# Layer 1's self-attention in a new order: queries half a head earlier, the last value matmul behind the next scores

## The chip, the cores and the metric

The kernel runs on one core of one Trainium2 chip. A core has five engines that each work through a queue of their own in order: TensorE (PE, with the weight load PEld), VectorE (DVE), ScalarE (ACT), GpSimd (POOL) and SyncE (SP, which here only starts transfers). They wait for each other through semaphores. The metric is the device time of one execution in microseconds (us); of several runs the median is given.

## The reference

The program is a decoder of two layers with layer normalisation after each residual addition. The residual x is 4 batches x 512 positions x 512 features in float32. Layer 0 has self-attention with 8-wide heads, a cross-attention and a mixture of eight experts; layer 1 has self-attention, cross-attention with 32 heads, and a quantised gated FFN. The change touches layer 1's self-attention alone:

```python
xqkv = x @ Wqkv                                  # 512 -> 16 query heads, 4 key heads, 4 value heads of 128
xq, xk = apply_rotary_emb(xq), apply_rotary_emb(xk)
xk, xv = repeat(xk, 4), repeat(xv, 4)            # four query heads share one key and value head
scores = einsum('bqhd,bkhd->bhqk', xq, xk) * 128 ** -0.5 + causal_mask
attn = einsum('bhqk,bkhd->bqhd', softmax(scores), xv)
x = layernorm(x + attn.reshape(B, S, 2048) @ Wo)
```

## The kernel before

The residual lies in SBUF for the whole run, as 16 tiles X[t] of 128 positions x 512 features. `l1_attn` (from line 887) takes 64 heads in order, 16 for each of the four batches, and works with the residual of a batch turned round: `st["xt"]`, features by positions, made by `transposed` (L258, 16 transposes of 128x128, copied by ACT and DVE in turn, L262 and L260).

For one head n these are the steps:

- `queries(n, i)` (L933): four matmuls, i = 0 to 3, each adding 128 features, into one PSUM bank of `ps_m`; after the last one `rope` rotates: three DVE operations (L903 to L905) and one POOL addition (L906). `keys(n)` does the same for every fourth head, all in one (L160 and `rope`).
- `scores(n, qi)` (L946): a matmul for the 128 queries qi against the (qi + 1) * 128 keys that the causal mask leaves, so 512, 384, 256 or 128 columns; then mask (L947) and negated maximum (L948) on DVE, and the exponential with its sum on ACT (L950).
- `normalise(n, qi)` (L956, L957): reciprocal and multiplication on DVE, SBUF to SBUF.
- `turn(n, c)` (L963): transposes of the probabilities' block column c into a bank of `ps_t`, copied to the tile PT by ACT for even c (L968), by DVE for odd c (L966).
- `values(n, pts)` (L978): four matmuls over PT into a bank of `ps_m`, copied by ACT (L980) to one quarter of the tile attnT; after every fourth head `add_projection` multiplies by Wo (16 matmuls, L160) and DVE adds to X (L313).

A float32 matmul shows in the trace as two, so a "pair" in this document is one matmul of the program. PSUM has three banks for scores (`ps_s`), two for transposes (`ps_t`), three for all else (`ps_m`).

The main loop has three heads in flight: in head n it transposes the probabilities of n and multiplies them by the values, computes the scores of n + 1, and the queries of n + 2. Its four inner steps are scores, one query matmul, one turn; `values` follows whole. At the end of a head come, where they are due: the next batch's transposes (`h == 13`), `at_start` (for n = 0, 1, 2: `finish(n + 1)`, the last part of layer 0's FFN for batch n + 1: scaling on ACT and DVE, L867 and L868, transposes L872, `add_projection` with 8 matmuls, layer normalisation), `at_end` (the first steps of the cross-attention, in the last five heads), and after the 16th head `layernorm` and `prep_values`.

The order in which an engine sees the instructions is fixed when the program is built. In this stage a scheduler sets it: an instruction may overtake others on its engine when they are not ready by the scheduler's own reckoning, with the order of the program as the priority. So in the kernel before, the first query matmul or key matmul of the next head often stands ahead of a head's last value matmul. The cross-attention behind the stage, in turn, is written out in a fixed order by a table of steps (`plan`, `todo`), which the change leaves alone.

Of the kernel before, what the change touches and what calls it, by code (L numbers as in the profile page):

```python
# [17 lines left out]
P = 128  # L18
B, S, F = 4, 512, 512
# [67 lines left out]
def decoder_kernel(ctx: ExitStack, tc: tile.TileContext, a: dict, out: bass.AP):  # L87
# [21 lines left out]
    V, A, G, PE = nc.vector, nc.scalar, nc.gpsimd, nc.tensor  # L109


    def act(tag, free, bufs=1, dtype=F32):
        return ap.tile([P, *free], dtype, tag=tag, name=tag, bufs=bufs)
# [13 lines left out]
    def pst(dtype=F32):  # L127
        if "ps_t" not in pools:
            return psm(dtype)
        return pools["ps_t"].tile([P, 512], dtype, tag="t", name="ps_t")  # L130

    def psm(dtype=F32):
        return pools["ps_m"].tile([P, 512], dtype, tag="m", name="ps_m")
# [16 lines left out]
    def tk(t):  # L150
        return slice(t * P, (t + 1) * P)
# [15 lines left out]
    ident = kc[:, C_ID:C_ID + P]  # L167
# [22 lines left out]
    X = []  # L190
# [55 lines left out]
    def layernorm(b):  # L246
        for i in range(4):
            tile_moments(b, i)
        table_roots(b)
        for i in range(4):  # L250
            normalise_tile(b, i)

    def transposed(b):
        xt = act("xT", [4, S])
        for k in range(4):
            pt = pst()
            for t in range(4):
                PE.transpose(pt[:, tk(t)], X[4 * b + t][:, tk(k)], ident)  # L258
            if k % 2:
                V.tensor_copy(xt[:, k, :], pt)  # L260
            else:
                A.copy(xt[:, k, :], pt)  # L262
        return xt
# [44 lines left out]
    def add_projection(b, lhs, rhs):  # L308

        for t in range(4):  # L310
            ps = psm()
            mm(ps, [x[:, tk(t)] for x in lhs], rhs)
            V.tensor_tensor(X[4 * b + t], X[4 * b + t], ps, ALU.add)  # L313

    def chunks(w):
        return [w[:, k, :] for k in range(w.shape[1])]
# [5 lines left out]
    def l0_attn(xt0):  # L322
# [82 lines left out]

        N = len(pairs)
        for n in range(2):
# [8 lines left out]
        for n, (b, m) in enumerate(pairs):  # L416
            for step in range(4):
                turn(n, step, 0)
                if n + 1 < N:
                    scores(n + 1, step)  # L420
                turn(n, step, 1)
                if n + 2 < N:
                    project(n + 2, step)
                if n + 1 < N and step:
                    normalise(n + 1, step - 1)
# [3 lines left out]
            values(n)  # L429
            if n + 1 < N:  # L430
                normalise(n + 1, 3)
# [455 lines left out]
    def l1_attn(at_start, at_end):  # L887
        cos, sin = prob("cos", [S], 1), prob("sin", [S], 1)
        causal_mask = prob("mask", [P], 1)
        nc.sync.dma_start(causal_mask, a["k_cols"][:, C_MASK:C_MASK + P])  # L890
        nc.sync.dma_start(cos, a["k_rope"][0])
        nc.sync.dma_start(sin, a["k_rope"][1])
        wqkv = rows(a["L1_attn_Wqkv"])
        wk = load(wqkv[:, :, 4 * F:5 * F], (4, F))
        wv = load(wqkv[:, :, 5 * F:6 * F], (4, F))
        wq, wo = [None] * 4, [None] * 4
        for of, g in ((wq, 0), (wq, 1), (wo, 0), (wq, 2), (wo, 1), (wq, 3), (wo, 2), (wo, 3)):
            src = wqkv[:, :, g * F:(g + 1) * F] if of is wq else rows(a["L1_attn_Wo"])[:, 4 * g:4 * g + 4, :]
            of[g] = load(src, (4, F))

        def rope(dst, ps, scale):
            x, y = tmp(), tmp()
            V.scalar_tensor_tensor(x, ps, scale, cos, ALU.mult, ALU.mult)  # L903
            V.scalar_tensor_tensor(y[0:64], ps[64:128], scale, sin[64:128], ALU.mult, ALU.mult)
            V.scalar_tensor_tensor(y[64:128], ps[0:64], scale, sin[0:64], ALU.mult, ALU.mult)  # L905
            G.tensor_tensor(dst, x, y, ALU.add)  # L906

        heads = [(b, h) for b in range(B) for h in range(H1)]  # L910
        st, qs, ks, ps_q, ps_sm = {}, {}, {}, {}, {}

        def prep_values(b):
            v = prob("v", [4, F], 1)
            for t in range(4):
                ps = psm()
                mm(ps, [st["xt"][:, k, tk(t)] for k in range(4)], chunks(wv))
                A.copy(v[:, t, :], ps)
            st["v"] = v

        def keys(n):
            b, h = heads[n]
            if h % 4 == 0:
                ps = psm()
                mm(ps, [wk[:, k, tk(h // 4)] for k in range(4)], chunks(st["xt"]))
                ks[b, h // 4] = prob("k", [S], 3)
                rope(ks[b, h // 4], ps, 1.0)

        def queries(n, i):
            b, h = heads[n]  # L930
            if i == 0:
                ps_q[n] = psm()
            PE.matmul(ps_q[n], lhsT=wq[h // 4][:, i, tk(h % 4)], rhs=st["xt"][:, i, :],  # L933
                      start=(i == 0), stop=(i == 3))
            if i == 3:
                qs[n] = prob("q", [S], 3)
                rope(qs[n], ps_q.pop(n), float(D1) ** -0.5)

        def scores(n, qi):
            b, h = heads[n]  # L940
            w, q, k = (qi + 1) * P, qs[n], ks[b, h // 4]
            if qi == 3:
                ps_sm[n] = [None] * 4, small(4, "sums", 3), small(4, "nmax", 3)
            probs, sums, nmax = ps_sm[n]
            s = pss()
            PE.matmul(s[:, :w], lhsT=q[:, tk(qi)], rhs=k[:, :w], start=True, stop=True)  # L946
            V.tensor_tensor(s[:, tk(qi)], s[:, tk(qi)], causal_mask, ALU.add)  # L947
            V.tensor_reduce(nmax[:, qi:qi + 1], s[:, :w], AX.X, ALU.max, negate=True)  # L948
            p = probs[qi] = prob("P", [S], 8)
            A.activation(p[:, :w], s[:, :w], AF.Exp, bias=nmax[:, qi:qi + 1],  # L950
                         accum_out=sums[:, qi:qi + 1])

        def normalise(n, qi):
            probs, sums, _ = ps_sm[n]
            p, w = probs[qi], (qi + 1) * P
            V.reciprocal(sums[:, qi:qi + 1], sums[:, qi:qi + 1])  # L956
            V.tensor_scalar(p[:, :w], p[:, :w], sums[:, qi:qi + 1], None, ALU.mult)  # L957

        def turn(n, c):
            probs = ps_sm[n][0]  # L960
            pt = pst()
            for qi in range(c, 4):
                PE.transpose(pt[:, tk(qi)], probs[qi][:, tk(c)], ident)  # L963
            sb = prob("PT", [S], 6)
            if c % 2:
                V.tensor_copy(sb[:, c * P:], pt[:, c * P:])  # L966
            else:
                A.copy(sb[:, c * P:], pt[:, c * P:])  # L968
            return sb

        def values(n, pts):
            b, h = heads[n]
            g = h // 4
            if h % 4 == 0:
                st["ft"] = act("attnT", [4, S])
            av = psm()
            for c in range(4):
                PE.matmul(av[:, c * P:], lhsT=st["v"][:, c, tk(g)], rhs=pts[c][:, c * P:],  # L978
                          start=(c == 0), stop=(c == 3))
            A.copy(st["ft"][:, h % 4, :], av)  # L980
            if h % 4 == 3:
                add_projection(b, chunks(st["ft"]), chunks(wo[g]))
            del ps_sm[n]

        N = len(heads)
        st["xt"] = transposed(0)
        for n in range(2):
            keys(n)
            for i in range(4):
                queries(n, i)  # L990
        for qi in (3, 2, 1, 0):
            scores(0, qi)
        prep_values(0)
        for qi in (3, 2, 1, 0):
            normalise(0, qi)
        for n, (b, h) in enumerate(heads):
            pts = []
            if n + 2 < N:
                keys(n + 2)
            for i in range(4):  # L1000
                qi = 3 - i
                if n + 1 < N:
                    scores(n + 1, qi)
                if n + 2 < N:
                    queries(n + 2, i)
                pts.append(turn(n, i))
                if n + 1 < N and i:
                    normalise(n + 1, qi + 1)
            values(n, pts)
            if n + 1 < N:  # L1010
                normalise(n + 1, 0)
            if h == 13 and b + 1 < B:
                st["xt"] = transposed(b + 1)
            if n < 3:
                at_start(n)
            if n >= N - 5:
                at_end(n - N + 5)
            if h == 15:
                layernorm(b)
                if b + 1 < B:  # L1020
                    prep_values(b + 1)

# [476 lines left out]
```

## Time and profile before

| | |
|---|---|
| median of 3 runs | 2916.74 us (2912.76 to 2916.99) |
| the profiled execution | 2925.97 us |
| its span, first to last instruction | 2924.2 us |
| mean granted TensorE clock | 0.983 |
| layer 1's self-attention, from its first key matmul to its last projection | about 980 to 1970 us |
| its queries, L933 | 512 matmul records, 261.4 us busy, 594 ns each |
| its scores, L946 | 512 matmul records, 183.3 us busy, 441 ns each |
| its values, L978 | 512 matmul records, 162.8 us busy, 441 ns each |
| DVE multiplication by the reciprocal, L957 | 256, 152.0 us busy, 594 ns each |
| POOL's last step of the rotation, L906 (queries) | 64, 82.0 us busy, 1281 ns each |

A row of a wait names the waiting engine, its tile and line, then the engine, tile and line that ended the wait; its numbers are the total in us, how many times, and the longest. A row of the timeline has start, duration, engine, line, operation, tiles and shape; "x2" merges two records, and brackets hold the idle time before and what ended it. A row of a stretch has the length, then for PE, PEld, DVE, ACT and POOL the busy time and the number of instructions, then PE's granted clock, the DMA engines' share and GB/s. A row of a group has its shape, the count, busy us and mean ns, and the idle time before.

### The profile page before, as it was taken

To read this page: it belongs to the slowest core of one execution; us is meant where nothing else is said; L and a number is where in the kernel's file an instruction comes from. 1 tells how busy PE (TensorE), PEld (TensorE's weight loads), DVE (VectorE), ACT (ScalarE), POOL (GpSimd) and SP (SyncE) were. 2 spreads that over 40 slices of the span, in tenths; PEclk is the share of its full clock that TensorE was granted. 3 is DMA by queue.
4 is the path that set the end of the run, shared out by engine and by line. 5 is a ranking of instruction groups with operands and counts; after the bars stand their busy time and mean duration, and the time that the engine had idled before them with its cause. 6 is when DMAs were issued, how large, how long until landed. Compare 5 with 4: busy or idle time off the path is not lost. (4 is left out here: it accounts for less than half of the span.)

```text
span 2924.2 us, 30438 instructions
## 1 busy us (share of the span) xinstructions
PE 2763.2 (94%) x11434; PEld 1347.8 (46%) x11434; DVE 1757.1 (60%) x3551; ACT 1046.8 (36%) x1929; POOL 425.0 (15%) x436
## 2 busy tenths in 40 slices
PE   8999999998998889999999999999999999998987
PEld 3444444565665345555555555553334334334443
DVE  4565564553111476767667666756656666565998
ACT  2333342333221122232233223234555554554443
POOL 3000000042002100111101101123333232211000
PEclk9999999999999899999999999999999999999999
DMA  9700000004322120000000001111111020010000
GB/s 386 278 15 1 15 4 27 23 29 137 101 85 97 35 87 1 1 0 1 1 1 1 1 0 44 58 47 38 56 55 58 37 86 27 12 51 1 15 15 30
DMA packets 61128, 142.76 MB, mean 49 GB/s; under 512 B 6537, under 2 KB 26010, under 8 KB 54818
## 3 DMA queue, kind: packets, MB, share of 16 engines
q1 hardware_dynamic: 54818, 123.80, 11.8%
q0 software_dynamic: 6144, 16.79, 1.6%
q8 instruction: 99, 1.62, 0.2%
q14 instruction: 67, 0.55, 0.1%
HBM read 84.73 MB, written 47.45 MB: 45 GB/s over the span
## 5 line engine op out<-in xcount | busy, mean ns | idle before, releaser
L1182 DVE TENSOR_REDUCE maxes<-ps_b 128x2 f32<-128x1024 f32 x256 | 312.6, 1223 | 212.0 <-PE ps_b L1194 113.8
L160 PE MATMUL ps_m<-w,attnT 128*128 128x512 f32 (+1 forms) x992 | 391.8, 547 | 9.7 <-DVE x L313 9.7
L1198 ACT ACTIVATE PT<-ps_b 128x1024 f32<-128x1024 f32 x256 | 260.3, 1023 | 237.0 <-PE ps_b L1194 236.9
L1178 PE MATMUL ps_b<-k,q 32*128 32x512 f32 x1024 | 287.0, 642 | 6.8 <-ACT PT L1198 6.8
L1194 PE MATMUL ps_b<-q,k 32*128 32x512 f32 x1024 | 285.5, 642 | 1.4 <-DVE maxes L1182 1.4
L933 PE MATMUL ps_m<-xT,w 128*128 128x512 f32 x512 | 261.4, 594 | 0.0
L313 DVE TENSOR_TENSOR x<-x,ps_m 128x512 f32<-128x512 f32 x128 | 87.8, 687 | 284.5 <-PE ps_m L160 257.1
L160 PEld LDWEIGHTS ps_m<-w,attnT 128*128 128x128 f32 x736 | 141.2, 195 | 177.3 <-issue 162.8
L950 ACT ACTIVATE P<-ps_s,nmax 128x512 f32<-128x512 f32 (+3 forms) x256 | 135.4, 529 | 234.9 <-DVE nmax L948 233.8
L946 PE MATMUL ps_s<-k,q 128*128 128x512 f32 (+3 forms) x512 | 183.3, 441 | 19.1 <-POOL q L906 17.4
L906 POOL TENSOR_TENSOR q<-tmp 128x512 f32<-128x512 f32 x64 | 82.0, 1281 | 765.8 <-DVE tmp L905 731.2
L978 PE MATMUL ps_m<-PT,v 128*128 128x512 f32 (+3 forms) x512 | 162.8, 441 | 4.0 <-DVE PT L966 4.0
L370 ACT ACTIVATE P<-ps_s,nmax 128x512 f32<-128x512 f32 x128 | 88.5, 693 | 203.5 <-DVE nmax L368 203.5
L957 DVE TENSOR_SCALAR P<-P,sums 128x512 f32<-128x512 f32 (+3 forms) x256 | 152.0, 594 | 5.3
L1178 PEld LDWEIGHTS ps_b<-k,q 32*128 32x128 f32 x1024 | 76.5, 183 | 155.2 <-issue 141.1
L160 PE MATMUL ps_m<-w,xT 128*128 128x512 f32 (+1 forms) x384 | 143.8, 530 | 3.4 <-DVE v L338 3.4
L1205 PE MATMUL ps_m<-PT,vv 128*32 128x512 f32 x1024 | 137.5, 609 | 7.5 <-ACT PT L1198 7.5
L963 PEld LDWEIGHTS ps_t<-kc,P 128*128 128x128 f32 x640 | 84.0, 141 | 121.3 <-issue 82.0
L978 PEld LDWEIGHTS ps_m<-PT,v 128*128 128x128 f32 x512 | 89.0, 190 | 106.1 <-issue 48.8
L348 PE MATMUL ps_m<-xT,w 128*128 128x512 f32 x256 | 122.3, 605 | 10.4 <-DMA w<-in_L_attn_Wq 10.4
L948 DVE TENSOR_REDUCE nmax<-ps_s 128x1 f32<-128x512 f32 (+3 forms) x256 | 125.5, 490 | 5.6
L947 DVE TENSOR_TENSOR ps_s<-ps_s,mask 128x128 f32<-128x128 f32 x256 | 75.1, 294 | 81.1 <-PE ps_s L946 78.9
(281 smaller groups left out, 4403.7 us busy)
## 6 DMA issues: line engine op xcount, KB each, us to landing
hidden<-w SPq DMA_DIRECT2D x16, 1024.0 KB, 16.7
result<-w SPq DMA_DIRECT2D x16, 1024.0 KB, 16.3
w<-in_L_ffn_gateT SPq DMA_DIRECT2D x8, 1024.0 KB, 4.8
tmp<-tmp POOLq DMA_DIRECT2D x64, 128.0 KB
w<-in_L_ffn_upT SPq DMA_DIRECT2D x8, 1024.0 KB, 4.8
w<-in_L_ffn_downT SPq DMA_DIRECT2D x8, 1024.0 KB, 5.5
w<-in_L_attn_Wqkv SPq DMA_DIRECT2D x6, 1024.0 KB, 8.9
w<-in_L_attn_Wo SPq DMA_DIRECT2D x5, 1024.0 KB, 13.6
```

The costliest lines, as they stand in the source:

```text
L160: PE.matmul(ps, lhsT=x, rhs=y, start=(i == 0), stop=(i == n - 1))
L933: PE.matmul(ps_q[n], lhsT=wq[h // 4][:, i, tk(h % 4)], rhs=st["xt"][:, i, :], start=(i == 0), stop=(i == 3))
L946: PE.matmul(s[:, :w], lhsT=q[:, tk(qi)], rhs=k[:, :w], start=True, stop=True)
L948: V.tensor_reduce(nmax[:, qi:qi + 1], s[:, :w], AX.X, ALU.max, negate=True)
L950: A.activation(p[:, :w], s[:, :w], AF.Exp, bias=nmax[:, qi:qi + 1], accum_out=sums[:, qi:qi + 1])
L957: V.tensor_scalar(p[:, :w], p[:, :w], sums[:, qi:qi + 1], None, ALU.mult)
L978: PE.matmul(av[:, c * P:], lhsT=st["v"][:, c, tk(g)], rhs=pts[c][:, c * P:], start=(c == 0), stop=(c == 3))
L1178: PE.matmul(s[:, j, :], lhsT=q[strip(i), tk(qi)], rhs=k[strip(i), :], start=True, stop=True)
L1182: V.tensor_reduce(at[:, 2 * half:2 * half + 2, 16 * (1 - g % 2)], s, AX.X, ALU.max, negate=True)
L1194: PE.matmul(s[:, j, :], lhsT=k[strip(i), tk(c)], rhs=q[strip(i), :], start=True, stop=True)
L1198: A.activation(p, s, AF.Exp)
L1205: PE.matmul(avs[g][strip(i), :], lhsT=vv[c][:, 4 * m + i, 16 * par:16 * par + 32], rhs=pts[g, c, i // 2][:, i % 2, :], start=(c == 0), sto ...
```

## The change

Four things are moved; what is computed stays the same.

- The queries run half a head further ahead. Before the loop two query matmuls of the third head are issued, and inner step i issues query matmul (i + 2) % 4 of head n + 2 + i // 2: in head n the last two of head n + 2, then the first two of head n + 3.
- `values` becomes a generator: it issues the first three value matmuls and stops; the rest (last value matmul, copy, projection, and after the 16th head layer normalisation and the next batch's values) runs in the next head, behind its first scores.
- The next batch's transposes move from the end of the 14th head into its last two inner steps, two groups of four in each, through a new function `turn_residual`.
- `layernorm` and `prep_values` move from the loop into `values`.

The diff (a hunk that adds one empty line is left out):

```diff
@@ -971,28 +972,51 @@
         def values(n, pts):
             b, h = heads[n]
             g = h // 4
+            av = psm()
+            for c in range(4):
+                if c == 3:
+                    yield
+                PE.matmul(av[:, c * P:], lhsT=st["v"][:, c, tk(g)], rhs=pts[c][:, c * P:],
+                          start=(c == 0), stop=(c == 3))
             if h % 4 == 0:
                 st["ft"] = act("attnT", [4, S])
-            av = psm()
-            for c in range(4):
-                PE.matmul(av[:, c * P:], lhsT=st["v"][:, c, tk(g)], rhs=pts[c][:, c * P:],
-                          start=(c == 0), stop=(c == 3))
             A.copy(st["ft"][:, h % 4, :], av)
             if h % 4 == 3:
                 add_projection(b, chunks(st["ft"]), chunks(wo[g]))
+            if h == 15:
+                layernorm(b)
+                if b + 1 < B:
+                    prep_values(b + 1)
             del ps_sm[n]
 
+        def turn_residual(b, k):
+            if k == 0:
+                st["xt"] = act("xT", [4, S])
+            pt = pst()
+            for t in range(4):
+                PE.transpose(pt[:, tk(t)], X[4 * b + t][:, tk(k)], ident)
+            if k % 2:
+                V.tensor_copy(st["xt"][:, k, :], pt)
+            else:
+                A.copy(st["xt"][:, k, :], pt)
+
         N = len(heads)
-        st["xt"] = transposed(0)
+        for k in range(4):
+            turn_residual(0, k)
         for n in range(2):
             keys(n)
             for i in range(4):
                 queries(n, i)
+        for i in range(2):
+            queries(2, i)
         for qi in (3, 2, 1, 0):
             scores(0, qi)
         prep_values(0)
         for qi in (3, 2, 1, 0):
             normalise(0, qi)
+
+
+        rest = iter(())
         for n, (b, h) in enumerate(heads):
             pts = []
             if n + 2 < N:
@@ -1001,24 +1025,26 @@
                 qi = 3 - i
                 if n + 1 < N:
                     scores(n + 1, qi)
-                if n + 2 < N:
-                    queries(n + 2, i)
+                if i == 0:
+                    next(rest, None)
+                if h == 13 and b + 1 < B and i >= 2:
+                    turn_residual(b + 1, 2 * i - 4)
+                    turn_residual(b + 1, 2 * i - 3)
+                if n + 2 + i // 2 < N:
+                    queries(n + 2 + i // 2, (i + 2) % 4)
                 pts.append(turn(n, i))
                 if n + 1 < N and i:
                     normalise(n + 1, qi + 1)
-            values(n, pts)
+            rest = values(n, pts)
+            next(rest)
             if n + 1 < N:
                 normalise(n + 1, 0)
-            if h == 13 and b + 1 < B:
-                st["xt"] = transposed(b + 1)
+            else:
+                next(rest, None)
             if n < 3:
                 at_start(n)
             if n >= N - 5:
                 at_end(n - N + 5)
-            if h == 15:
-                layernorm(b)
-                if b + 1 < B:
-                    prep_values(b + 1)
```

## Prediction

> **What bounds the kernel now.** I read the page's first part, then stretches of the span, then TensorE's waits inside the changed stage, then the timeline of one head. The first line says that TensorE (PE) is busy for nearly the whole span; the stretches show that this holds inside layer 1's self-attention (about 975 to 1970 us) too:
>
> ```profile
> PE 2763.2 (94%) x11434; PEld 1347.8 (46%) x11434; DVE 1757.1 (60%) x3551; ACT 1046.8 (36%) x1929; POOL 425.0 (15%) x436
> ...
> 975.00:1110.00 135.00, 119.72 (x338) 57.68 (x337) 83.51 (x190) 35.55 (x80) 10.39 (x8) 0.95 0.16 55
> 1110.00:1960.00 850.00, 831.78 (x2762) 440.42 (x2761) 576.99 (x1380) 254.16 (x689) 103.14 (x84) 1.00 0.04 12
> ```
>
> From 1110 to 1960 us PE is busy for 831.78 of 850 us at clock 1.00, so a change of order, with the same matmuls, can win little more than the holes. Who ends the holes, in that stretch and then in 975 to 1110 us:
>
> ```profile
> PE ps_s L946 <- POOL q L906: 16.6, 29, 0.6
> PE ps_m L978 <- DVE PT L966: 1.2, 4, 0.3
> ...
> PE ps_t L963 <- ACT PT L968: 5.2, 2, 3.3
> PE ps_t L872 <- DVE w L868: 3.4, 2, 1.7
> PE ps_m L978 <- DVE PT L966: 2.8, 4, 1.0
> ```
>
> The first score matmul of every second head waits for its rotated queries. In one such head, PE first, then VectorE (DVE):
>
> ```profile
> 1316.89 2.10 PE L978 MATMUL ps_m<-PT,v 128*128 128x512 f32 x6
> 1318.83 1.02 PE L933 MATMUL ps_m<-xT,w 128*128 128x512 f32 x2
> 1319.69 0.38 PE L978 MATMUL ps_m<-PT,v 128*128 128x128 f32 x2
> 1320.64 1.13 PE L946 MATMUL ps_s<-k,q 128*128 128x512 f32 x2 [0.57 <-POOL q L906]
> 1321.60 0.60 PE L963 MATMUL ps_t<-kc,P 128*128 128x128 f32 x4
> ...
> 1317.05 0.69 DVE L903 SCALAR_TENSOR_TENSOR tmp<-ps_m,cos 128x512 f32<-128x512 f32 x1
> 1318.46 0.68 DVE L905 SCALAR_TENSOR_TENSOR tmp<-ps_m,sin 64x512 f32<-64x512 f32 x1
> 1319.18 0.29 DVE L966 COPY PT<-ps_t 128x128 f32<-128x128 f32 x1
> 1319.38 1.35 DVE L957 TENSOR_SCALAR P<-P,sums 128x256 f32<-128x256 f32 x1
> 1321.80 0.30 DVE L947 TENSOR_TENSOR ps_s<-ps_s,mask 128x128 f32<-128x128 f32 x1 [0.68 <-PE ps_s L946]
> ```
>
> The last query matmul of the coming head is issued at the head's end; three DVE operations (1317.05 to 1319.14) and POOL's 1.27 us addition follow, and scores cannot start before 1320.64. Starts tell more than the idle column, because matmul ends are modelled: a pair of 128-column matmuls takes 0.22 us from start to start (that at 1303.24 is followed at 1303.46), here 0.95. So 0.73 us is lost, and the score pair itself takes 0.96 instead of 0.86: 0.83 us a time. The rotation stands ahead of the 128-column copy of PT as well, which is why the last value matmul comes late.
>
> **The change, part by part.** In the changed kernel no matmul, vector operation, copy or DMA is added or removed; PE's order differs, and with it that of DVE and ScalarE (ACT).
>
> *Queries half a head ahead: gain 25.7 us.* The last query matmul of a head is now its second of four, about half a head before the scores that need it. The wait of L946 for POOL happens 31 times (29 in the long stretch, 2 before): 31 x 0.83 = 25.7. If only the idle of the row goes, 17.4; that is the lower end.
>
> *Last value matmul behind the next scores: gain 6.5 us.* Its wait for PT is short: at 1306.37 a pair starts, the value pair follows at 1307.30 where 1307.23 was due, and takes 0.32 where 0.22 is due, 0.17 in all. Some 30 heads make 5; the rows of 2.8 and 1.2 us contain a few long ones, so I put 6.5 (ends 4 and 9). What now hides the copy is the 0.86 us score pair. If this cover is gone, the 0.17 us returns, and the waiting matmul holds up the projection of every fourth head, which stands behind it on PE.
>
> *DVE in the heads without key or output projection, two in four: cost 2.4 us.* Here PE needs: 3.44 for four query pairs, 2.16 scores, 2.16 values, 1.1 for ten transposes, 8.86 us. By start-to-start steps DVE needs four masks 1.32, four maxima 1.64, reciprocals 0.76, normalisations 1.21, rotation 2.11, copies 0.67, together 7.71, and it must wait about 0.95 for the first exponential of the head, which stands before the second mask in the new order: 8.66. I followed one such head by hand: the copy of PT ends 0.5 us ahead of the last value matmul, the last normalisation 0.6 ahead of the first transpose. So it just fits. After a key projection DVE starts the next head 1.25 us late and misses the value matmul by about 0.15: 16 groups x 0.15 = 2.4. With full durations instead of steps (8.21 + 0.97 = 9.18 us) each light head loses 0.32 less some slack, 0.5 a group, 8 us: the upper end; the lower is 0.
>
> [...] The row:
>
> ```profile
> L957 DVE TENSOR_SCALAR P<-P,sums 128x128 f32<-128x128 f32 x59 | 50.3, 853 | 2.1
> L957 DVE TENSOR_SCALAR P<-P,sums 128x256 f32<-128x256 f32 x59 | 37.9, 642 | 1.1
> ```
>
> The shortest 128x128 takes 285 ns, an undisturbed 128x256 350: while POOL adds, DVE loses 0.57 + 0.29 = 0.86 us a head. [...] If the row's 0.86 stays and falls on the last normalisation, its 0.6 us of slack is overrun by 0.26, 64 times: 17 us, and the sum below would be 0. [...]
>
> *PSUM banks in the first two heads: cost 6.7 us.* ps_m has three. Across the head's end the half-built queries now hold one and the unfinished values another; finish(1) and finish(2) project between, four tiles through one bank, and each tile waits for DVE's addition to the tile before. One gap: 0.20 from the end of a matmul stream to DVE (1321.60 to 1321.80), 0.69 addition (row L313), 0.22 back to PE (copy end 1319.47 to 1319.69) = 1.11. Three gaps twice: 6.7. Ends 3 (the queue of PE hides part) and 9 (DVE is delayed further). For finish(3) values and scores interleave with its transposes: 2 us, ends -1 and 5.
>
> *The same two heads otherwise: gain 3, cost 1.6.* The rotation no longer stands before DVE's scaling of w (L868), for which PE waits 3.4 us: 3 gained, ends 0 and 6. The PT copy of the second transpose now stands behind the rotation while DVE is catching up after layer normalisation: 0.8 twice lost.
>
> *Batch ends: cost 4.5 us.* The 16 transposes of the next batch's residual move into the 14th head and share two ps_t banks with the probabilities; four of them wait for a copy, and the first query matmul behind them waits for ACT. The nearest row, the old transposes, lost about 0.5 a time; four waits of 0.5, less the old one, make 1.5, three times. Ends 0 and 9. Layer normalisation and the values of the next batch move one score pair later: 0, hidden behind 16 matmul pairs of 0.86 us. The three or four last heads have half a head of queries less to fill them while DVE limits: 1, ends 0 and 1.7.
>
> The DMAs and POOL's operations stay in their order. The sum: -25.7 - 6.5 - 3 + 2.4 + 6.7 + 2 + 1.6 + 4.5 + 1 = -17.0. The cross-attention's order behind is the same and PE leads there too, so the whole stage moves forward. The profiled execution took 2925.97 (span 2924.2), 9.2 above the median of 2916.74; its span should become 2907, the median 2916.7 - 17.0 = 2899.7, in round numbers 2900.
>
> [...] The page's row of clocks has all tenths but one at 9 here, yet the stretch 975 to 1110 has 0.95: 0.05 x 135 = 7 us of clock lost already. [...] I take 0 and keep 7 for the range.
>
> **The rivals.**
> *A wait takes its place (0.15).* The first transposes of a head then wait for the last normalisation as scores did for queries; half of the 25.7 is lost, 2912.6 at most, 2909 if some of the batch-end cost hides. For: 6.9 us of weight loads already wait for L957. Against: 0.6 us of slack by hand.
> *DVE becomes the bound (0.12), slower.* [...] It decides once a light head's DVE chain exceeds 8.86 + 17/32 = 9.4 us. Against: DVE was busy for 577 of 850 us, blocking included.
> *Nothing moves (0.05), 2917.* The time returns at the cross-attention's start, which waits for loads. Against: PE has no DMA wait there, and those loads move at 0.13 to 0.18 of the DMA engines.
> *All new costs hide (0.08).* -25.7 - 6.5 = -32: 2885.
>
> **How the numbers follow.** My sum has 0.60, with its own range 2892 to 2908 (its unknown terms added as independent). A measurement tells 0.2%, 5.8 us, from no change: faster is below 2910.9. Faster: 0.60 + 0.08 + about half of the 0.15 = 0.75; same: the rest of it and 0.05 = 0.13; slower 0.12. The range runs from 2885 to 2914, leaving out the slower rival and small ends.
>
> **What would show it.** The row L946 <- POOL q near 0; L957 128x128 near 300 ns; new rows of L160 (ctx) waiting for DVE x before 1070 us, about 7 us; waits of the batch-end transposes; 1110 to 1960 shorter by some 25 us. Wrong it is if L963 waits for P in most heads, or if L979's wait for PT grows in the light heads.

## The result and the profile after

The changed kernel takes 2880.96 us (median of 4 runs, 2878.24 to 2889.82), the kernel before beside it 2916.23 (4 runs): ratio 0.9887, 95% interval 0.9864 to 0.9909. That is 35.3 us less. The prediction had the sign right and the size wrong: 2900, with a range down to 2885. The profiled execution took 2881.12 us, its span 2879.3.

TensorE's and VectorE's totals, and the same two stretches of the span (columns: stretch, length, then busy time of PE, weight loads, DVE, ACT and POOL with their instructions, PE clock, DMA share, GB/s):

```profile
PE 2747.5 (95%) x11434; PEld 1347.1 (47%) x11434; DVE 1700.2 (59%) x3551; ACT 1048.1 (36%) x1929; POOL 427.3 (15%) x436
...
975.00:1110.00 135.00, 120.51 (x352) 58.31 (x351) 86.38 (x216) 39.88 (x98) 9.95 (x8) 0.94 0.13 47
1110.00:1960.00 850.00, 846.96 (x2863) 449.69 (x2861) 532.27 (x1377) 261.70 (x686) 125.25 (x109) 1.00 0.04 15
```

In the long stretch PE is now busy for 846.96 of 850 us (831.78 before), and the cross-attention behind the stage begins at 1928 us instead of 1975. The stretch thus holds 32 us of cross-attention now; in what is left of it, 1110 to 1928 us, PE is busy for 815.4 of 818. DVE's total fell from 1757.1 to 1700.2 us with the same 3551 instructions.

TensorE's waits in 1110 to 1960 us, and then in 975 to 1110 us:

```profile
PE ps_t L997 <- ACT xT L1001: 1.4, 3, 0.5
PE ps_m L1152 <- DVE x L313: 0.8, 1, 0.8
...
PE ps_m L160 <- DVE x L313: 5.5, 7, 0.8
PE ps_t L964 <- ACT PT L969: 4.7, 2, 3.6
PE ps_m L979 <- ACT PT L969: 1.6, 2, 0.9
PE ps_t L872 <- DVE w L868: 1.2, 2, 1.0
```

(Lines of the stage moved by 1, the part behind it by 26: the scores are now L947, the normalisation L958.) The row of scores waiting for POOL's q, 16.6 us in 29 waits, is gone. New are the predicted waits of L160 for the additions to x in the first heads, 5.5 us in 7, and one wait of 0.5 at each batch end.

One head of the changed kernel, the one behind that which answers to the head shown before (some rows left out), PE first, then DVE:

```profile
1302.01 1.02 PE L934 MATMUL ps_m<-xT,w 128*128 128x512 f32 x2
1302.87 0.27 PE L964 MATMUL ps_t<-kc,P 128*128 128x128 f32 x1
1302.98 2.10 PE L979 MATMUL ps_m<-PT,v 128*128 128x512 f32 x6
1304.92 1.02 PE L947 MATMUL ps_s<-k,q 128*128 128x512 f32 x2
1305.77 0.38 PE L979 MATMUL ps_m<-PT,v 128*128 128x128 f32 x2
...
1300.56 0.68 DVE L903 SCALAR_TENSOR_TENSOR tmp<-ps_m,cos 128x512 f32<-128x512 f32 x1
1301.96 0.68 DVE L905 SCALAR_TENSOR_TENSOR tmp<-ps_m,sin 64x512 f32<-64x512 f32 x1
1304.47 0.28 DVE L967 COPY PT<-ps_t 128x128 f32<-128x128 f32 x1
1305.31 0.29 DVE L958 TENSOR_SCALAR P<-P,sums 128x128 f32<-128x128 f32 x1
1305.97 0.30 DVE L948 TENSOR_TENSOR ps_s<-ps_s,mask 128x128 f32<-128x128 f32 x1 [0.37 <-PE ps_s L947]
```

The rotation ends at 1302.64, and POOL's 1.30 us addition, which starts at 1302.82, at 1304.12; the scores follow the third value pair at 1304.92 without a hole. The copy of PT is over at 1304.75, the value pair that needs it starts at 1305.77. DVE then stands idle for 0.37 us: it waits for PE.

### The profile page after: what moved, and what is told of

Read it like the earlier page. It is cut to its first block, busy times and chain, and to the rows that moved or that the text cites. A ratio compares the mean times of both kernels' runs of the same rounds, so it can differ in the third digit from the quotient of the medians.

```text
span 2879.3 us, 30399 instructions
## 1 busy us (share of the span) xinstructions
PE 2747.5 (95%) x11434; PEld 1347.1 (47%) x11434; DVE 1700.2 (59%) x3551; ACT 1048.1 (36%) x1929; POOL 427.3 (15%) x436
## 5 line engine op out<-in xcount | busy, mean ns | idle before, releaser
L160 PE MATMUL ps_m<-w,attnT 128*128 128x512 f32 (+1 forms) x992 | 383.4, 541 | 0.0
L313 DVE TENSOR_TENSOR x<-x,ps_m 128x512 f32<-128x512 f32 x128 | 87.9, 687 | 259.0 <-PE ps_m L160 258.9
L160 PEld LDWEIGHTS ps_m<-w,attnT 128*128 128x128 f32 x736 | 139.5, 192 | 169.5 <-issue 164.9
L906 POOL TENSOR_TENSOR q<-tmp 128x512 f32<-128x512 f32 x64 | 83.3, 1302 | 694.3 <-DVE tmp L905 622.5
L947 PE MATMUL ps_s<-k,q 128*128 128x512 f32 (+3 forms) x512 | 180.1, 434 | 0.9 <-ACT P L951 0.9
L969 ACT COPY PT<-ps_t 128x512 f32<-128x512 f32 (+1 forms) x128 | 61.0, 476 | 238.9 <-PE ps_t L964 238.9
L160 PE MATMUL ps_m<-w,xT 128*128 128x512 f32 (+1 forms) x384 | 143.8, 530 | 3.2 <-DVE v L338 3.2
L964 PEld LDWEIGHTS ps_t<-kc,P 128*128 128x128 f32 x640 | 83.6, 141 | 121.0 <-issue 79.2
L348 PE MATMUL ps_m<-xT,w 128*128 128x512 f32 x256 | 122.1, 604 | 10.2 <-DMA w<-in_L_attn_Wq 10.2
L160 PE MATMUL ps_m<-PT,w 128*128 128x512 f32 (+1 forms) x248 | 114.4, 590 | 7.5 <-PEq L833 3.6
```

The costliest lines, as they stand in the source:

```text
L160: PE.matmul(ps, lhsT=x, rhs=y, start=(i == 0), stop=(i == n - 1))
L348: PE.matmul(acc[n], lhsT=w[:, k, tk(m)], rhs=st["xt"][:, k, :], start=(k == 0), stop=(k == 3))
```

## The experiments

A ratio below is always to the kernel before, run on the same chip between the others. "The stage" is the time from its first score matmul to the cross-attention's first one. Code is shown in excerpts.

**Both kernels once more.** No edit. One thing in the first pair of profiles needed an answer: of the 44.9 us between the spans, only 29.9 lie in the stage (984.5 against 954.6); 16.7 lie ahead of it, and 1.8 are given back behind it.

> The kernel before, unchanged, profiled once more. In the first pair of profiles 16.7 us of the difference arose ahead of the stage: in layer 0's finish(0), at 940 to 970 us, VectorE's additions of L313 came 4 to 9 us late with no releaser that the profile names. Theory: the lateness varies from execution to execution, and the profiled one, 9.2 above the median, had some 9 us more of it than the others. Then the first score matmul of the stage (990.3 before, 973.6 after) comes at about 981 here, the time is 2916, and 7 of the median's -35.3 us lie ahead of the stage. Rival: the lateness is fixed to the old order; then 990 again, with the same L313 rows. Second rival: it was one accident; then 974, and the whole median difference arises in the stage.

> The changed kernel, unchanged, profiled once more. If the lateness of L313 is a matter of the execution alone, it can appear here too (first score matmul of the stage anywhere from 974 to 990 us, the time moving with it, as the 2889.8 among the runs of 2878 to 2881 would suggest); if it is tied to the old order, the first score comes at 974 again and the time is 2881. In both cases the stage, from its first score to the cross-attention's first pass, takes 954 to 955 us, against 984 to 985 for the kernel before.

Measured: ratio 1.0002 (0.9989 to 1.0015) and 0.9886 (0.9853 to 0.9919). The first score comes at 973.9 and 976.5 us; the stage takes 985.0 and 954.6. A small part of these 30.3 us is no gain: the change issues two query matmuls ahead of the first scores, and so ahead of the mark where the stage starts. From the first query matmul on (966.67 and 967.91 us) the kernel before takes 992.2, the changed one 963.2, which is 29.0 less.

VectorE's waits of L313 from 935 to 990 us in the first profile of the kernel before:

```profile
DVE x L313 <- remote: 19.6, 3, 9.1
DVE x L313 <- issue: 7.6, 2, 4.9
```

The new profile of the same kernel has neither row, nor have the three others of this series. A later profile of the changed kernel has them (900 to 980 us):

```profile
DVE x L313 <- remote: 17.0, 3, 8.5
DVE x L313 <- issue: 2.7, 1, 2.7
```

In the two later series, in which the kernel before took 2929 to 2932 us, all seven profiles have such rows and start the stage at 990 us or later, whatever their order in the stage. The lateness, then, is not tied to the old order, and what a comparison made side by side carries is the stage's 30 us. What holds VectorE there stays open: the profile names no releaser, and no run was made for it. The chip itself is a candidate: the four profiles of this series come from one chip and the seven later ones from another, and the changed kernel has the rows on the second and not on the first. For the first pair the chip is not on record.

**The queries alone.** The changed kernel, with the four value matmuls together as before:

```
 for c in range(4):
-    if c == 3:
-        yield
     PE.matmul(av[:, c * P:], ...)
...
-rest = values(n, pts)
-next(rest)
+values(n, pts)
```

> One part alone: the queries half a head further ahead, with the transposes of the batch ends that they need; the four value matmuls stay together, as before. By my sum: -25.7 for the queries, +4.5 batch ends, -3 +1.6 in the first heads, +1 at the tail, and only one ps_m bank held across finish(1) and finish(2): -20, 2896. If the whole gain inside the stage was the queries' (rival: the values' part is worth nothing), the stage takes 954 us and the time is near 2881 to 2886. If the values' part was worth more than 6.5, the stage stays above 965.

Measured: ratio 0.9896 (0.9869 to 0.9923), stage 954.0 us. So -31 us in the stage, not the expected -20, and as much as the whole change. That is a balance: from the scores of head 14 to those of head 62 the whole change takes 679.4 us and this kernel 681.9, so there the later value matmul is worth 2.6 us; in the first 14 heads the whole change takes 3.0 us more.

**The values alone.** The kernel before, with the last value matmul behind the next scores:

```
+rest = iter(())
 for n, (b, h) in enumerate(heads):
...
         scores(n + 1, qi)
+        if i == 0:
+            next(rest, None)
...
-    values(n, pts)
+    rest = values(n, pts)
+    next(rest)
```

> The other part alone: the last value matmul behind the next head's first scores, queries as before. By my sum -6.5, with one ps_m bank more held across finish(1) and finish(2) +3, so 2910 to 2914. Rival: the order of DVE's work at the head's end matters more than the wait for PT, because the score matmul there still waits for the rotated queries, and then the value matmul only waits behind it: no gain, 2917. Either way the row of scores waiting for POOL's q stays near 16.6 us x 29.

Measured: ratio 1.0084 (1.0056 to 1.0113), 25 us slower; stage 1011.4. Neither theory had it. TensorE's first wait in the stage, in the kernel before (its new profile) and then in this one:

```profile
PE ps_s L946 <- POOL q L906: 17.9, 31, 0.6
```

```profile
PE ps_s L946 <- POOL q L906: 45.0, 50, 1.3
```

Two things that stood between the queries and the scores, and so covered the rotation, are gone. The last value matmul, 0.22 us and its own wait for PT, is missing in the 31 heads that waited before: their waits grow from 17.9 to 26.9 us. And in one head of four the projection, which stands behind that matmul on PE, went with it. Such a head before (first three rows), then in this run:

```profile
1309.32 1.02 PE L933 MATMUL ps_m<-xT,w 128*128 128x512 f32 x2
1313.48 13.04 PE L160 MATMUL ps_m<-w,attnT 128*128 128x512 f32 x30
1326.36 1.02 PE L946 MATMUL ps_s<-k,q 128*128 128x512 f32 x2
...
1317.30 1.02 PE L933 MATMUL ps_m<-xT,w 128*128 128x512 f32 x2
1322.26 1.13 PE L946 MATMUL ps_s<-k,q 128*128 128x512 f32 x2 [1.04 <-POOL q L906]
1323.44 13.04 PE L160 MATMUL ps_m<-w,attnT 128*128 128x512 f32 x30
```

These heads did not wait before; now 15 of them wait for 15.9 us together. With four more at the batch ends and at the end of the stage (2.3 us) that makes 50 waits instead of 31. The second half of the change pays only behind the first.

**How much lead?** The changed kernel with a quarter head instead of half a one:

```
-if n + 2 + i // 2 < N:
-    queries(n + 2 + i // 2, (i + 2) % 4)
+if n + 2 + i // 3 < N:
+    queries(n + 2 + i // 3, (i + 1) % 4)
```

(with the transposes at the batch ends in the head's last quarter, and one query matmul instead of two ahead of the loop).

> The changed kernel with its queries a quarter of a head ahead in place of half a head (the last query matmul of a head is third of four). My theory: the scores waited for the rotation by 0.83 us a time, and a quarter head is about 2.2 us, so the row of scores waiting for POOL's q stays near 0 and the stage takes 955 us, the time 2881, as with half a head. [...] Rival: the slack of VectorE is what half a head buys, and then the stage takes 960 to 970 us. If the lead had to be half a head to clear the wait, some of the 16.6 us row comes back.

Measured: ratio 1.0016 (1.0004 to 1.0027), stage 988.2: the whole gain is gone. The scores' waits in the stage, then one head, PE and DVE (some rows left out):

```profile
PE ps_s L947 <- POOL q L906: 23.1, 46, 0.8
```

```profile
1302.21 1.02 PE L934 MATMUL ps_m<-xT,w 128*128 128x512 f32 x2
1306.92 1.13 PE L947 MATMUL ps_s<-k,q 128*128 128x512 f32 x2 [0.34 <-POOL q L906]
...
1302.78 0.42 DVE L949 TENSOR_REDUCE nmax<-ps_s 128x1 f32<-128x256 f32 x1
1303.34 0.69 DVE L903 SCALAR_TENSOR_TENSOR tmp<-ps_m,cos 128x512 f32<-128x512 f32 x1
1304.75 0.68 DVE L905 SCALAR_TENSOR_TENSOR tmp<-ps_m,sin 64x512 f32<-64x512 f32 x1
1305.55 0.28 DVE L948 TENSOR_TENSOR ps_s<-ps_s,mask 128x128 f32<-128x128 f32 x1
1305.73 1.35 DVE L958 TENSOR_SCALAR P<-P,sums 128x384 f32<-128x384 f32 x1
```

From the last query pair to its scores 4.71 us pass: 0.86 the pair itself, 0.27 until DVE is free, 2.09 of rotation, 1.43 to the end of POOL's addition (1306.86), 0.06 to PE. I had compared the lead of 2.2 us with the hole of 0.83 that it was to fill; but the matmuls between the last query pair and the scores (1302.21 to about 1306.4) cover less than that chain, the more so because the old order's value matmul, and in one head of four the projection, no longer stand in front of the scores. With half a head, 5.83 us lie between the two starts (1299.09 and 1304.92 in the head shown for the changed kernel), about a microsecond more than the chain. Normalisations that run beside POOL's addition take longer here again: in this head POOL runs from 1305.60 to 1306.86, the 128x384 normalisation that starts inside it takes 1.35 us instead of 0.41 (as the next one does, at 1312.74), and the mask at 1305.55 its usual 0.28. Over the stage the 128x256 normalisations take 640 ns in the mean, against 354 in the first run of the held-bank experiment.

Then three quarters of a head (with three query matmuls ahead of the loop, the batch ends' transposes in the last three quarters of the head, and the edit of the next paragraph, with which it is to be compared):

```
+if n + 2 + (i > 0) < N:
+    queries(n + 2 + (i > 0), (i + 3) % 4)
```

> The same as the last one, but with queries three quarters of a head ahead (the last query matmul of a head is its first). In the run with a quarter, 4.7 us passed from the last query matmul to the scores that it let go: about 1.1 until VectorE got to it, 2.1 of rotation, 1.3 of POOL; half a head gives 5.7, so there is 0.8 to 1.0 us to spare. My theory: the lead works like a threshold, and more of it buys nothing: stage 949 to 950 us, same time as with half a head. Rival: the rotation now stands ahead of the first PT copy and the 128x512 normalisation, and POOL's addition blocks that normalisation, so the first transposes of the next head or the value matmuls wait: 5 us or more slower.

Measured: ratio 0.9852 (0.9836 to 0.9869), stage 945.3, 5.7 less than its partner's 951.0 on the same chip. For the steady heads the threshold holds: from the scores of head 6 to those of head 14 the changed kernel, this one and its partner take 105.1 us each, against 109.3 before. The 5.7 us come from the irregular places: 2.9 in the first heads, 0.6 at each batch end, 1.1 in the last two heads (where 0.9 is one query matmul less, now issued ahead of the stage's start). No new wait appears, so the rival is out.

**The held PSUM bank.** The changed kernel, but the first three heads finish their values before finish(1) to finish(3):

```
 if n < 3:
+    next(rest, None)
     at_start(n)
```

> The changed kernel, but in the first three heads the last value matmul is issued at the head's end, ahead of finish(1) to finish(3), so that no unfinished value tile holds a ps_m bank across them. My theory: the waits of L160 (ctx) for VectorE's additions to x (5.5 us in 7) and the half us lost at each beside them go, 6 us of starts in all, and the last value matmul of two heads waits for its PT copy again, 2.5 us as in the kernel before. The stage takes 951 us against 954.6, the time is some 3.5 us shorter than the changed kernel's, 2877. Rival: the gaps lay within VectorE's own lateness after layer normalisation, and what goes there comes back in the next wait for PT: 954.6 and 2881.

Measured: ratio 0.9877 (0.9860 to 0.9893), stage 949.4. L160 no longer waits for L313, as expected. In place of the expected 2.5 us of waiting for PT, L872 waits 3.4 us for w again (1.2 in the changed kernel). Timed over five rounds beside the changed kernel:

> The changed kernel once more, timed on the same chip as the next two, so that a few us between them can be told. Stage 954.6 us, ratio to the kernel before 0.9885 to 0.989. The gain by heads, from the first scores of one head to those of a later one, is 2.0 us for each four heads again, also across the batch ends (there 1.7 to 1.8), as in the profile taken before: my sum had 32.2 / 16 = 2.0 for the queries and values, but took 1.5 back at each batch end and 0.15 in each four heads.

> The changed kernel with the value matmuls of the first three heads kept together, timed over five rounds. The stage took 949.4 us in its first profile, 5.2 less than the changed kernel's: 949 to 950 again, and a time 3 to 5 us below the changed kernel's, ratio 0.987. If the waits at finish(1) and finish(2) came back elsewhere, its time equals the changed kernel's.

Measured: 0.9900 (0.9881 to 0.9918) for the changed kernel, 0.9878 (0.9861 to 0.9894) for this one; stages 951.8 and 951.0. The intervals overlap, and the stages were 0.8 us apart this time, not 5.2. The clock, which the last section shows, can account for that: in the first 100 us of the stage its mean was 0.91 and 0.95 in the two profiles of the changed kernel, 0.95 and 0.93 in those of this one. With the loss taken off (an estimate: 100 us times what is missing to 1.00), this one is some 2 us shorter in both pairs. That it is the better one is likely, not settled.

**How near is VectorE to the bound?** The changed kernel with one, then two multiplications of 128x512 more in each head, their result unused:

```
 rope(qs[n], ps_q.pop(n), float(D1) ** -0.5)
+junk = tmp()
+for _ in range(1):
+    V.tensor_tensor(junk, cos, sin, ALU.mult)
```

> The changed kernel with one VectorE multiplication of 128x512 more after each head's query rotation, its result unused: 0.69 us, 64 times, 44 us of VectorE in all. It asks how near VectorE is to the bound. By the prediction's sum a light head of VectorE takes 8.66 us of 8.86, so 0.49 us is missing in each of 32 light heads, 16 us slower than the changed kernel (2897). By the trace of the changed kernel VectorE has 0.37 us to spare in a light head, and the copy of PT and the last normalisation come 0.8 and 1.2 us ahead of need, a store that every fourth head fills again: 0.32 us a head is taken from it for two or three heads, at most 0.1 us is missing in each of 16 groups: 2881 to 2884.

> The same with two such multiplications, 1.38 us in each head, 88 us of VectorE in all. By the trace's 0.37 us to spare, 1.0 us a head is missing for three heads, 3.0 us, of which the store takes 0.8 to 1.2: some 2 us in each of 16 groups, 30 us, 2911. By the prediction's sum 1.2 us is missing in each of 32 light heads, 38 us, 2919. If VectorE had no part in the bound at all the time would stay at 2881.

Measured: 0.9895 (0.9878 to 0.9912), stage 957.3, which is 2.7 more than the changed kernel's 954.6 and 5.5 more than the 951.8 of its third profile, whose clock in the first 100 us was the same 0.95; and 1.0022 (1.0012 to 1.0031), stage 993.9, 39.3 more than 954.6. So 44 us of added VectorE work (704 ns a multiplication in the trace) cost 3 to 6 us. Two in each head, put at 88 us, are 128.4 us in the trace (126 records, 1019 ns in the mean), and cost about 40. With two multiplications PE waits for VectorE 44 times, for PT and for the normalised P:

```profile
PE ps_m L982 <- DVE PT L970: 8.9, 29, 0.3
...
PE ps_t L967 <- DVE P L961: 4.4, 15, 1.1
```

For one, the count from the trace's 0.37 us and the store of lead (at most 3) came near, and the 8.66 of 8.86 us in the prediction left too little (16). For two, the total is what the prediction's sum gave (38), but by luck: from head 14 to head 62, where all is regular, 24.1 us were lost, 2.0 in each four heads, which is the trace's count. The other 15 were lost in the first 14 heads (11.6) and the last two (3.6), which neither count looked at. The addition is not quite clean: with one multiplication POOL's 98 operations of the stage take 25.8 us more (last section).

## Why the prediction was right in sign and wrong in size

To compare term by term, I take the start-to-start steps of all matmuls of the stage, subtract from each the commonest step of its width, and add up what is left by pairs of lines. In the new profile of the kernel before this makes 60.2 us, in that of the changed one 31.4 us. The rest of the stage's 30.3 is for the most part the two query matmuls that now stand ahead of the stage's start.

| step of the prediction | predicted | measured |
|---|---|---|
| queries half a head ahead (holes in front of the scores and in the score pair: 28.1 to 1.3) | -25.7 | -26.8 |
| last value matmul, and DVE in the light heads (holes in front of and among value matmuls: 9.5 to 3.8) | -6.5 + 2.4 | -5.7 |
| PSUM banks, finish(1) to finish(3) (holes among L160, ctx: 4.0 to 10.1) | +6.7 + 2 | +6.1 |
| their transposes and L868 (8.2 to 4.3) | -3 | -3.9 |
| PT copy of the second transpose (6.0 to 5.8) | +1.6 | -0.2 |
| batch ends (1.5 to 1.9) | +4.5 | +0.4 |
| tail | +1 | none seen |
| sum | -17.0 | -30.1 |

The sums still contain matmuls at half the clock (last section), by an estimate from the profile's clock records 6.1 and 7.0 us, and not in the same rows: of the PSUM row's 4.0 and 10.1 they are 3.5 and 3.4, of the value row's 9.5 and 3.8 they are 0.3 and 1.5. Without them the values gained some 7 us. The PSUM waits cost 6.2, and 7.2 with the last of the seven, whose step leads to another line and is not in the row. The 0 that the prediction took for a further loss of clock is shown by no run, and neither is a further loss of the 7 us that it kept for the range; the runs show a mean clock of 0.93 over the first 100 us of the stage before, and of 0.91 to 0.95 after.

*Queries: right*, in size and reason. The row is gone, and the starts gave back 26.8 over 31 waits, 0.86 us each where 0.83 was put. Twelve groups of four heads, from the scores of head 14 to those of head 62, gained 24.0 us, 2.0 each with three batch ends among them; -25.7 and -6.5 over 16 groups are 2.0.

*Values: right as a sum, but not by itself.* The prediction treated the two parts as independent. The runs show -31 us in the stage for the first alone, +26 for the second alone, and -30 together. What it left out is that the projection leaves the place in front of the scores together with the value matmul.

*Light heads: the failed step was "misses the value matmul by about 0.15".* By hand I had found 0.5 us of slack for the copy of PT and 0.6 for the last normalisation; in the head before the one shown, which follows a key projection, they are 0.39 and 0.61 (the copy ends at 1296.53 and the last normalisation at 1297.39; the value pair starts at 1296.92, the transposes at 1298.00). Nothing is missed, and in the head shown the copy has 1.02. DVE has room for nearly all of another 0.69 us a head, which cost 2.7 us in 48 heads.

*The 0.86 us a head that VectorE loses while POOL adds* (the "blocking" of the slower rival) was rightly left out of the sum. That the new order would end it was my estimate; what makes the normalisations longer is shown by no run, only when they are longer: in the first profile of the kernel before, the 61 of 128x128 and 128x256 that overlap an addition of the rotation (L906) take 1.07 to 1.38 us, and the 67 others 0.28 to 0.35. The row of the changed kernel:

```profile
L958 DVE TENSOR_SCALAR P<-P,sums 128x128 f32<-128x128 f32 x64 | 18.3, 286 | 2.2
```

286 ns, where the prediction's row had 853; DVE's total is 57 us less, and 64 x 0.86 is 55. The loss is not gone everywhere: in 18 heads the 128x512 normalisation takes 0.9 us or more instead of 0.49 (0.99 at 1294.22, while POOL adds from 1293.63 to 1294.93), 9 us in all, and PE does not wait for it. In the quarter-head run it is there too, 1.35 us for 0.41 in the head shown.

*Batch ends: the failed step was "four of them wait for a copy".* One of them does, at each batch end, for 0.5 us, and the old transposes lost as much. *PSUM banks: right in kind and nearly in size*, seven waits, where I had six gaps and 2 us for finish(3); by the starts about 1.0 us each, where 1.11 was put, 7.2 without the clock instead of 8.7. Keeping the value matmuls together removed those waits.

So no single term accounts for the 13 us: every cost that I could not read from a row was put above nothing, and nearly all were covered. That is the rival "all new costs hide", 2885, to which I gave 0.08, except that the PSUM waits stayed and finish gained a little more. I had added my unknown terms as independent; they had one cause in common, how much slack each head has, and so they failed together. Slack of 0.5 us read by hand should have made them small together, and the lower end of the range should have held all of them at nothing: -25.7 - 6.5 - 3 = -35.2, 2881.5, where I stopped at 2885.

The first comparison's -35.3 us is 5 more than the stage's 30; with 30 alone the time would have been 2886, just inside the range, so that it fell below 2885 is in part chance. The repetitions on one chip each gave ratios of 0.9886 and 0.9900, with intervals that hold 0.9896, which is 30 us; no part outside the stage is shown to have changed.

*The slower rival* needed 9.4 us of DVE chain in a light head. With 0.69 us more, which by the prediction's 8.66 is 9.35, the loss was 2.7 to 5.5 us; with 1.38, which is 10.04 (10.7 by the 1019 ns of the trace), it was 39.3. The point at which 17 us are lost lies between, at 9.4 or above it, and the changed kernel stands more than half a microsecond a head short of it. *"A wait takes its place"* did not happen: in neither list of waits of the changed kernel does L964 wait for P.

## What to carry to other kernels

A lead must be at least the whole chain from the last input to the consumer (here 4.7 us: the pair, DVE's queue, rotation, POOL), not the hole seen in the trace; here the gain was nothing about half a microsecond short of it, and whole a microsecond beyond. When a matmul is moved, look at what stands behind it in the same queue and moves with it, since that may have been the cover of another wait: here one move alone was 25 us slower, and the two together were not the sum of both. And costs that hang on the same slack go to nothing together, so the range must reach to the case where all of them do.

## What the runs showed of the hardware

*Half the clock behind a partly idle stretch.* The prediction took 0 for any further loss of clock. In the changed kernel's first profile, then in its third (columns as in the first fence of stretches):

```profile
996.00:999.00 3.00, 3.00 (x12) 1.25 (x10) 2.90 (x7) 0.02 (x1) 1.30 (x1) 1.00 0.01 3
999.00:1002.00 3.00, 1.20 (x5) 0.54 (x4) 2.86 (x12) 2.77 (x9) 0.00 (x0) 0.97 0.00 0
1002.00:1012.00 10.00, 9.22 (x15) 3.55 (x15) 2.83 (x5) 1.37 (x2) 0.00 (x0) 0.50 0.32 107
```

```profile
1016.00:1019.00 3.00, 1.27 (x4) 0.30 (x2) 2.86 (x12) 2.34 (x8) 0.00 (x0) 1.00 0.00 0
1019.00:1020.00 1.00, 0.88 (x3) 0.46 (x3) 1.00 (x3) 0.98 (x3) 0.00 (x0) 0.86 0.00 0
1020.00:1023.00 3.00, 3.00 (x8) 1.77 (x8) 1.58 (x3) 0.84 (x1) 0.00 (x0) 0.50 0.14 37
```

PE was busy for 1.20 and 1.27 of 3 us, in pieces, and the clock fell to 0.50: for 10 us in one execution, for a little over 3 in the other, at the same place of the program. In the five profiles of the two kernels such stretches of the stage last about 3.4, 6.8 or 10.2 us, and they differ from one execution to the next. In the first of the two profiles shown the longest hole ahead of the fall was 1.04 us. What makes the clock fall no run shows. At a clock of 0.50 a 512-column matmul of L160 took 0.86 us from start to start (1009.59 to 1010.45 in the first profile), at 1.00 it took 0.43 (1013.59 to 1014.02). The 7 us at half the clock that one execution has more are worth about 3.4 us of PE's work, by an estimate from these two steps; the third profile's stage is 951.8 and not 954.6, and 2.7 of these 2.8 us lie in the second head, where this stretch is. That is also why one profile each could not tell the kernel with the held bank from the one without. The kernel before has such stretches at the same place (0.77 of the clock from 1000 to 1015 us in its new profile). Over the first 100 us of the stage its mean clock is 0.93 in both profiles, the changed kernel's 0.91, 0.91 and 0.95, so the change as a whole lost or gained at most 2 us by it.

*VectorE and POOL side by side.* In the quarter-head run, while POOL's addition ran, a normalisation between SBUF tiles took 1.35 us for 0.41, a mask on PSUM 0.28 as ever. Not every overlap costs time: the changed kernel's 128x384 normalisation at 1303.94, which starts 0.18 us before the end of POOL's addition (1304.12), takes 0.41. POOL's operations can be the longer ones: its 98 of the stage were busy for 143.8 us with one added VectorE multiplication in each head, both inputs in SBUF, and for 118.0 in the first run of the held-bank experiment, which is 0.4 us more for each of 64 heads.
